# Four products of a block's last state, spread over the first step of the next block

## The chip, the cores and the metric

The kernel runs on one core of one Trainium2 chip. The metric is the device time of one execution in microseconds (us). A core has five engines that run side by side and wait for each other by semaphores: TensorE (matrix products, "PE" in the profile, its weight loads "PEld"), VectorE ("DVE"), ScalarE ("ACT"), GpSimd ("POOL") and SyncE ("SP"), from whose queue nearly all transfers of this kernel are issued, one after the other. Each engine takes its instructions in program order, so one that waits holds up all behind it.

## The reference, cut to what matters

Two layers follow each other; the change is in the second one, a gated recurrence. Its input `x` has 8 rows in time and 2048 columns that are independent of each other (the recurrence calls them a batch), of width 512.

```
def step(c, xt):
    ft = sigmoid(xt @ wf.T + c @ uf.T + bf)
    it = sigmoid(xt @ wi.T + c @ ui.T + bi)
    gt = tanh(xt @ wc.T + c @ uc.T + bc)
    c = ft * c + it * gt
    return (c, None)
c_final, _ = lax.scan(step, c0, x)
h = tanh(einsum('tbi,oi->tbo', x, wo) + c_final @ uo.T + bo)
out = x + layernorm(h)
```

The state after the last step, `c_final`, enters every row of the output by one product with `uo`. That product, plus the bias `bo`, is what the change moves. The first layer (a state-space convolution, a gelu and a layer norm) takes the time up to about 680 us and is not touched.

## The kernel before

**Blocks and steps.** The 2048 columns are cut into four blocks `q` of 512. Each block runs through 8 steps `t`, so there are 32 steps `n = 8q + t`, one after the other. A step has eight units: two `z` units (the product of `x` with `wo`, independent of the state), then six gate units (gates 1, 2, 0 for the first half of the outputs, then gates 1, 2, 0 for the second half). The products are computed by a scheme with seven instead of eight block products, in pairs of f16 numbers (three matmuls for each f32 product). At `t = 0` the initial state is the same for all columns, its product is part of the bias, and the gate units have no state part: 24 matmuls in a unit's first half and 18 in its second. At `t > 0` a gate unit has twice as many.

**Order.** The order of every engine's work is written by hand. Slot `sl` of step `n` calls `part_a` of its unit (first 24 or 48 matmuls, then sums from the result tile by ScalarE and VectorE: `u2`, `c22`, `u[:, 2:4]`), then whatever was put at place `p = 16n + 2 sl`, then `part_b` of the unit before (the other matmuls, then either the copy of a `z` result to memory, L973 to L980, or the gate functions on ScalarE, L987, and for gate 0 the new state in `state`, L1007 to L1020), then whatever was put at `p + 1`. In every step but the first the second half of `z1` is held back by one slot (`late`). The state is written as f16 pairs `cf0`, `cf1`, for the two halves; `cf1` is the last thing that a step makes, and falls in the next step's first slots.

**Result tiles.** `pu` has three tiles `u` that units take in turn, so a unit's first matmul waits until an older unit's results have been read.

**Side work, with its places.** `prep` (load `y` and `xr`, layer norm statistics, scale, sum, store) prepares two steps of the input of one 128-column chunk; it holds the single tiles with the tags `y` and `wl`. 60 preparations are spread over the steps by `when`. `turn` loads the next step's input, normalises it, transposes it on TensorE (L485) and writes its forms `xf`. `head` makes the output rows of the block before, five or four to a step with `t > 0`: load `z`, add the state's product `u`, tanh, statistics, normalise, add `x1`, store. The last heads of a block reach into the next block's first step. `tail` does the same for the last block after the last step.

**The product of the last state.** `last(q - 1)` is put in the first step of block `q`. Its `load` (place 5) issues the bias `bo` and four weight tiles `uw`; its `sums` (place 7) takes two `u` tiles, runs all 60 matmuls (4 products, 512 wide, for the four chunks `cj`: 12, 12, 18 and 18) and has VectorE add the bias (L1056); its `store` (place 8) writes the four results, which the heads read back. After the last step `last(3)` runs the same without a store.

## Time and profile before

| | us |
|---|---|
| median of 3 runs (2947.64 to 2950.56) | 2949.14 |
| the profiled execution | 2952.36 |
| its span | 2950.6 |
| ordinary step at t > 0, blocks 1 to 3 (1627.96 to 1694.21) | 66.25 |
| first step of block 1 (1223.61 to 1297.96) | 74.35 |
| first step of block 2 (1760.45 to 1837.12) | 76.67 |
| first step of block 3 (2299.07 to 2376.22) | 77.15 |
| idle of TensorE ahead of the product, by a DMA, block 1 | 8.0 |

Steps are measured from the start of the first matmul of `z0` to the next step's. In the profile's rows, "x" gives a count of instructions, the mean duration is in ns, and after the bar stand the idle time of the engine just before such instructions and what ended it. Matmuls overlap, so a matmul's duration is longer than the time from one start to the next; where that matters, starts are compared.

### The profile page before, as it was taken

Reading aid. Unit: us, or ns where it says so; the run is one execution under the profiler, and the core shown is the slowest. Engines: PE = TensorE matmul, PEld = TensorE weight load, DVE = VectorE, ACT = ScalarE, POOL = GpSimd, SP = SyncE. Lnnn points to the kernel's source line nnn. Section 1 sums busy time; section 2 is a strip of 40 time slices with the busy share of each in tenths; the row PEclk is TensorE's granted clock in tenths of the full one; section 3 lists DMA queues with packets and bytes.
Section 4 is the critical chain, followed back from the end, with each engine's and each line's share of the span. In section 5 each row is a group of like instructions: output and inputs, shape, how many; then the busy total and the mean of one; then the engine's idle time right before and its main releaser. Section 6 shows DMA issues by size and latency. Waiting matters only on the chain.

```text
span 2950.6 us, 60067 instructions
## 1 busy us (share of the span) xinstructions
PE 2600.0 (88%) x23940; PEld 2262.3 (77%) x23940; DVE 2068.4 (70%) x4260; ACT 1487.0 (50%) x3076; POOL 1115.1 (38%) x1484
## 2 busy tenths in 40 slices
PE   4678888875899999899999997999999899999970
PEld 3367777764788888778888885888888688888850
DVE  8868778736666676667777776777777577777637
ACT  8856666633344444434555543445454345454425
POOL 5756677612111111114434331343433224333217
PEclk8789999986999999999999998999999999999985
DMA  6877887794433223334454444455545344543227
GB/s 240 287 223 248 252 259 245 236 269 164 129 94 80 72 72 89 102 107 132 138 148 136 129 119 122 108 154 150 153 121 136 108 125 136 138 129 113 82 107 278
DMA packets 517762, 452.15 MB, mean 153 GB/s; under 512 B 285926, under 2 KB 397032, under 8 KB 512488
## 3 DMA queue, kind: packets, MB, share of 16 engines
q1 hardware_dynamic: 517048, 447.79, 51.1%
q8 instruction: 187, 3.06, 0.4%
q14 instruction: 95, 0.78, 0.1%
q10 hardware_dynamic: 432, 0.52, 0.1%
HBM read 296.46 MB, written 151.78 MB: 152 GB/s over the span
## 4 chain that ended last, share of the span: by engine, by line
PE 55%; DVE 11%; ACT 4%; DMA 4%; issue 1%; POOL 1%; SPq 1%; POOLq 0%; ACTq 0%; DVEq 0%
PE u L921 51%; PE pt L485 2%; DVE cd L1008 1%; ACT xa L907 1%; DVE gate L1007 1%; DVE stx L462 1%; DVE u L963 1%; DMA zz<-z_d 1%; PE u L450 1%; DMA uw<-uo_d 1%; PE u L451 1%; PE u L452 1%; DVE gate L1011 1%; DMA z_d<-zc 1%; DVE sth L462 1%
## 5 line engine op out<-in xcount | busy, mean ns | idle before, releaser
L921 PEld LDWEIGHTS <-w 128*128 128x128 f16 x15120 | 1485.3, 98 | 204.8 <-issue 15.0
L921 PE MATMUL u<-xf,w 128*128 128x256 f16 x8064 | 953.3, 275 | 23.8 <-DVE u L963 10.5
L921 PE MATMUL u<-cf,w 128*128 128x256 f16 x7056 | 825.2, 273 | 0.0
L987 ACT ACTIVATE gate<-u,bias 128x512 f32<-128x512 f32 (+1 forms) x384 | 200.9, 575 | 267.6 <-PE u L921 267.6
L921 PE MATMUL u<-w,xf 128*128 128x256 f16 x2688 | 311.7, 274 | 8.7 <-DVE u L963 8.7
L1094 POOL TENSOR_TENSOR x1r<-x1r,zr 128x512 f32<-128x512 f32 x96 | 124.5, 1297 | 487.9 <-ACT zr L1093 400.3
L882 POOL TENSOR_TENSOR xr<-y,xr 128x512 f32<-128x512 f32 x120 | 150.9, 1279 | 399.7 <-ACT y L881 399.7
L921 PEld LDWEIGHTS <-xf 128*128 128x128 f16 x2688 | 264.0, 98 | 41.2 <-DVE u L963 9.5
L960 DVE TENSOR_TENSOR u2p<-u2p,u 128x256 f32<-128x256 f32 x256 | 107.0, 418 | 237.3 <-ACT u2p L959 236.8
L959 ACT ACTIVATE u2p<-u 128x256 f32<-128x256 f32 x256 | 96.4, 376 | 316.3 <-PE u L921 316.3
L471 POOL TENSOR_TENSOR rsy<-rsy,nhalf 128x2 f32<-128x2 f32 (+1 forms) x68 | 48.5, 714 | 513.5 <-DVE rsy L465 502.6
L963 DVE TENSOR_TENSOR u<-u,u2p 128x512 f32<-128x512 f32 x256 | 178.9, 699 | 8.8
L639 POOL TENSOR_TENSOR u<-xg,u 128x512 f16<-128x512 f32 x104 | 128.6, 1240 | 124.6 <-ACT u L637 124.0
L633 POOL TENSOR_TENSOR xg<-xg,mu 128x512 f32<-128x512 f32 x112 | 162.3, 1456 | 9.5 <-DMA xg<-in_xr 9.5
L102 DVE TENSOR_TENSOR x<-pxt,x 128x256 f16<-128x256 f32 x240 | 99.9, 418 | 71.0 <-ACT x L101 69.9
L101 ACT ACTIVATE xf<-pt 128x512 f16<-128x512 f32 x124 | 60.8, 490 | 164.5 <-DVE ts L495 117.5
L1018 ACT ACTIVATE cf<-gate 128x512 f16<-128x512 f32 x128 | 80.7, 630 | 121.6 <-DVE gate L1011 103.1
L462 DVE BATCH_NORM_STATS2 sty<-y 128x6 f32<-128x512 f32 x120 | 76.8, 682 | 91.4 <-DMA y<-y_d 91.4
L101 ACT ACTIVATE x<-pxt 128x256 f16<-128x256 f32 x240 | 91.3, 381 | 80.7 <-PE pxt L659 74.6
L452 PE MATMUL pyt<-u,t 128*128 128x128 f16 (+2 forms) x544 | 124.7, 229 | 4.9 <-POOL u L615 4.9
L450 PE MATMUL pyt<-u,t 128*128 128x128 f16 (+2 forms) x544 | 121.6, 224 | 6.4 <-ACT y L738 3.4
L1076 POOL TENSOR_TENSOR zr<-zr,ur 128x512 f32<-128x512 f32 x96 | 122.1, 1272 | 9.1 <-DMA zr<-z_d 8.9
(349 smaller groups left out, 5279.5 us busy)
## 6 DMA issues: line engine op xcount, KB each, us to landing
xs<-in_rr SPq DMA_DIRECT2D x32, 1024.0 KB, 6.6
t<-kpad SPq DMA_DIRECT2D x32, 1024.0 KB, 5.7
xa<-x_d SPq DMA_DIRECT2D x124, 256.0 KB, 3.8
xr<-in_r SPq DMA_DIRECT2D x61, 512.0 KB, 6.5
x_d<-xr SPq DMA_DIRECT2D x61, 512.0 KB, 3.2
y_d<-y SPq DMA_DIRECT2D x30, 1024.0 KB, 7.5
y<-y_d SPq DMA_DIRECT2D x60, 512.0 KB, 5.7
xg<-in_xr SPq DMA_DIRECT2D x28, 1024.0 KB, 8.6
```

What stands on the lines that cost most here:

```text
L101: S.activation(hi, src, AF.Copy)
L450: T.matmul(out, lhsT=w(0), rhs=x(0), start=start, stop=False)
L452: T.matmul(out, lhsT=w(0), rhs=x(1), start=False, stop=stop)
L462: V.bn_stats(st[:, i], v)
L633: Q.tensor_tensor(xg, xg, bc(mu1), ALU.subtract)
L639: (V if g == 2 else Q).tensor_tensor(u[:, js, 1], xg, u[:, js, 0], ALU.subtract)
L882: Q.tensor_tensor(xv, yv, xv, ALU.add)
L921: T.matmul(u[:, d], lhsT=w(f, b, i == 1, k), rhs=x(f, b, i == 2, k), start=opens and bank not in seen, stop=stop and j == len(n) - 1, skip ...
L963: V.tensor_tensor(u[:, 2:4], u[:, 2:4], u2[:, None].to_broadcast([P, 2, BP]), ALU.add)
L987: act = lambda o, s_, b: S.activation(o, s_, AF.Tanh, scale=gsc[kind], bias=b)
L1076: Q.tensor_tensor(s_["z"], s_["z"], us_[c], ALU.add)
L1094: Q.tensor_tensor(s_["x"], s_["x"], s_["z"], ALU.add)
```

## The change

The product is cut into four, one for each chunk, each with a `u` tile of its own (except after the last step, where two chunks share one). Loads, four products and four results get places of their own: the weights at -2, which is in the last slot of the step before; the bias at 4; the products at 3, 5, 7 and 13; the results at 5, 7, 9 and 14; the store at 15. The weights now lie in the tiles of the preparations (tags `wl` and `y`), in two loads. The result is copied by ScalarE from the `u` tile, ScalarE scales the bias once, and GpSimd adds it; after the last step VectorE still adds it in place.

For this, the first step of a block has no preparations; the others are spread over the steps with `t > 0`, at new places: three of them at `t = 3` and `t = 5`, two at the others. In the first step of blocks 1 to 3 the turn is put earlier (0 to 10 in place of 2 to 13), and `z1` is no longer held back.

```diff
     def last(q):
-        end, uws, uo = q == NQB - 1, [], []
+        end, uws, uo, us = q == NQB - 1, [], [], {}
         def load():
-            bo = FT.tile([P, H], F32, name="bo", tag="x1r", bufs=2)
-            dma(out=bo, in_=a["bo"])
             if end:
                 u4 = FE.tile([P, KT, 2, H], F16, name="uw", tag="xf")
                 dma(out=u4, in_=uo_d.rearrange("k p a m -> p k a m"))
                 uws.extend(u4[:, k] for k in range(KT))
+                return
+            for i, (pool, tag) in enumerate(((FJ, "wl"), (FE, "y"))):
+                u2 = pool.tile([P, 2, 2, H], F16, name="uw", tag=tag)
+                dma(out=u2, in_=uo_d[2 * i : 2 * i + 2].rearrange("k p a m -> p k a m"))
+                uws.extend(u2[:, k] for k in range(2))
+        def load_b():
+            bo = FT.tile([P, H], F32, name="bo", tag="x1r", bufs=2)
+            dma(out=bo, in_=a["bo"])
+            uws.append(bo)
+        def sums(cj):
+            cf, i, cs = cfs[q, NB - 1], cj // 2, slice(cj % 2 * P, (cj % 2 + 1) * P)
+            if end and cj % 2:
+                u = us[cj - 1]
             else:
-                for k in range(KT):
-                    uw = FT.tile([P, 2, H], F16, name="uw", tag="zr", bufs=4)
-                    dma(out=uw, in_=uo_d[k])
-                    uws.append(uw)
-            uws.append(bo)
...
+                u = pu.tile([P, 4, BP], F32, name="u").rearrange("p (a b) c -> p a (b c)", a=2)
+            us[cj] = u
...
+        def out(cj):
+            p_ = us[cj][:, cj % 2]
+            if end:
+                V.scalar_tensor_tensor(p_, uws[KT], SW, p_, ALU.mult, ALU.add)
+                us_[QC * q + cj] = p_
+            else:
+                u_ = FT.tile([P, H], F32, name="u_", tag="zr", bufs=4)
+                S.activation(u_, p_, AF.Copy)
+                if cj == 0:
+                    S.mul(uws[KT], uws[KT], SW)
+                Q.tensor_tensor(u_, u_, uws[KT], ALU.add)
+                uo.append(u_)
...
-        return (load, sums) if end else (load, sums, store)
+        one = lambda f, cj: lambda: f(cj)
+        return [load, load_b] + [one(f, cj) for cj in range(QC) for f in (sums, out)] + ([] if end else [store])
...
-    PA, PB = (5, 7, 8, 10, 11), (12, 16, 17, 19, 20)
...
-    when += [(n, p) for n in range(2, len(steps)) for p in (PA, PB)]
+    PF, PL = ((1, 3, 4, 5, 6), (7, 9, 10, 11, 12)), ((5, 7, 8, 10, 11), (11, 13, 14, 15, 16))
+    PT = PF + ((13, 16, 17, 19, 20),)
+    when = [(0, p) for p in ((0, 2, 3, 4, 5), (5, 7, 8, 9, 10), (11, 13, 14, 15, 16))] + [(1, p) for p in PT]
+    for n, (q, t) in enumerate(steps):
+        if n > 1 and t:
+            when += [(n, p) for p in (PT if t in (3, 5) else PL if t in (4, 6) or n == 2 else PF)]
...
+        if q and t == 0:
+            put(last(q - 1), b, (-2, 4, 3, 5, 5, 7, 7, 9, 13, 14, 15))
         if n + 1 < len(steps):
+            ps = ((2, 5, 6, 7, 8), (9, 10, 11, 12, 13))
+            if t == 0:
+                ps = ((0, 1, 2, 3, 5), (6, 7, 8, 9, 10)) if n else ((0, 1, 2, 3, 4), (5, 6, 8, 9, 11))
             for i in range(2):
-                put(turn(*steps[n + 1], i), b, (((2, 5, 6, 7, 8), (9, 10, 11, 12, 13)) if n else ((0, 1, 2, 3, 4), (5, 6, 8, 9, 11)))[i])
+                put(turn(*steps[n + 1], i), b, ps[i])
...
-        if q and t == 0:
-            put(last(q - 1), b, (5, 7, 8))
...
-                late = n and sl == 2
-                if sl == 3 and n:
+                late = n and t and sl == 2
+                if sl == 3 and n and t:
                     finish(zs[1], p + 1)
                     before = gs[0]
```

More of the change, by code (lines that the diff above doesn't have):

```diff
@@ L1032, in load @@
                 uws.extend(u4[:, k] for k in range(KT))
-            else:
-                for k in range(KT):
-                    uw = FT.tile([P, 2, H], F16, name="uw", tag="zr", bufs=4)
-                    dma(out=uw, in_=uo_d[k])
-                    uws.append(uw)
-            uws.append(bo)
-        def sums():
-            cf = cfs[q, NB - 1]
-            uu = [pu.tile([P, 4, BP], F32, name="u").rearrange("p (a b) c -> p a (b c)", a=2) for _ in range(2)]
-            for cj in range(QC):
-                i, cs = cj // 2, slice(cj % 2 * P, (cj % 2 + 1) * P)
-                ps = [(k, b) for k in range(KT) for b in (((FB11,) if i == 0 else (FB11, FT1)) if k < 2 else ((FB21,) if i == 0 else (FB22,)))]
-                for n, (k, b) in enumerate(ps):
-                    mm3(uu[i][:, cj % 2], lambda l: cf[k % 2][:, b, l, cs], lambda l: uws[k][:, l],
-                        start=(n == 0), stop=(n == len(ps) - 1))
-            for cj in range(QC):
-                p_ = uu[cj // 2][:, cj % 2]
-                if end:
-                    us_[QC * q + cj] = u_ = p_
-                else:
-                    u_ = FT.tile([P, H], F32, name="u_", tag="zr", bufs=4)
-                    uo.append(u_)
-                V.scalar_tensor_tensor(u_, uws[KT], SW, p_, ALU.mult, ALU.add)
@@ new lines, in load @@
+                return
[11 more added lines that the diff above has]
+                u = us[cj - 1]
+            else:
+                u = pu.tile([P, 4, BP], F32, name="u").rearrange("p (a b) c -> p a (b c)", a=2)
+            us[cj] = u
+            ps = [(k, b) for k in range(KT) for b in (((FB11,) if i == 0 else (FB11, FT1)) if k < 2 else ((FB21,) if i == 0 else (FB22,)))]
+            for n, (k, b) in enumerate(ps):
+                mm3(u[:, cj % 2], lambda l: cf[k % 2][:, b, l, cs], lambda l: uws[k][:, l],
+                    start=(n == 0), stop=(n == len(ps) - 1))
@@ L1164, in s4_gated_block @@
     chunks = [(g, cj) for g in range(1, len(pairs)) for cj in (0, 2, 1, 3)]
-    PA, PB = (5, 7, 8, 10, 11), (12, 16, 17, 19, 20)
-    when = [(0, (0, 2, 3, 4, 5)), (0, (5, 7, 8, 9, 10)), (0, (11, 13, 14, 15, 16)),
-            (1, (1, 3, 4, 5, 6)), (1, (7, 9, 10, 11, 12)), (1, (13, 16, 17, 19, 20))]
-    when += [(n, p) for n in range(2, len(steps)) for p in (PA, PB)]
+    PF, PL = ((1, 3, 4, 5, 6), (7, 9, 10, 11, 12)), ((5, 7, 8, 10, 11), (11, 13, 14, 15, 16))
[4 more added lines that the diff above has]
+            when += [(n, p) for p in (PT if t in (3, 5) else PL if t in (4, 6) or n == 2 else PF)]
     for n, (q, t) in enumerate(steps):
```

## The prediction

> **What bounds the kernel now.** I read the page first, then the steps of the recurrence one by one (from the first matmul of a step's unit z0 to that of the next step), then the chain of waits and the timelines inside the steps that the diff touches.

> ```profile
> span 2950.6 us, 60067 instructions
> PE 2600.0 (88%) x23940; PEld 2262.3 (77%) x23940; DVE 2068.4 (70%) x4260; ACT 1487.0 (50%) x3076; POOL 1115.1 (38%) x1484
> L921 PE MATMUL u<-cf,w 128*128 128x256 f16 x7056 | 825.2, 273 | 0.0
> ```

> TensorE is the busiest engine, and its recurrent products never wait. Next, busy time by stretch: the three first steps of blocks 1 to 3, then an ordinary step (columns: stretch, length, then PE, PEld, DVE, ACT, POOL busy, clock, DMA).

> ```profile
> 1223.61:1297.96 74.35, 59.61 (x432) 44.43 (x430) 43.73 (x88) 27.11 (x56) 10.50 (x16) 0.89 0.38 110
> 1760.45:1837.12 76.67, 58.85 (x432) 43.97 (x430) 45.86 (x93) 28.71 (x58) 13.75 (x22) 0.89 0.44 130
> 2299.07:2376.22 77.15, 59.24 (x433) 44.16 (x430) 46.18 (x93) 28.92 (x58) 13.76 (x22) 0.89 0.45 129
> 1627.96:1694.21 66.25, 66.20 (x607) 59.23 (x605) 49.37 (x101) 32.86 (x64) 24.23 (x37) 1.00 0.47 132
> ```

> The ordinary step is TensorE's own work, at full clock (588 matmuls of 109.2 ns and two groups of transposes make 66.0). The first steps take 8 to 11 us more with 30% fewer matmuls. What they wait for is in the chain (start, length, what) and in TensorE's timeline; the bracket is the idle time before a row and its releaser.

> ```profile
> 1243.98 3.35 SPq L869
> ...
> 1247.37 0.47 SPq L1028
> ...
> 1247.88 4.42 DMA uw<-uo_d
> 1252.30 0.14 issue
> 1252.43 0.59 PE u L450
> 1253.02 0.43 PE u L451
> ```

> ```profile
> 1279.87 6.41 PE L921 MATMUL u<-xf,w 128*128 128x256 f16 x42 [2.09 <-ACT gate L987]
> 1290.74 1.82 PE L485 MATMUL pt<-cst,xa 128*128 128x128 f32 x8 [4.46 <-ACT xa L907]
> 1292.35 5.78 PE L921 MATMUL u<-xf,w 128*128 128x256 f16 x42
> ```

> ```profile
> 2357.63 2.78 PE L921 MATMUL u<-xf,w 128*128 128x256 f16 x24 [1.80 <-ACT gate L987]
> 2360.86 2.14 PE L921 MATMUL u<-xf,w 128*128 128x256 f16 x18 [0.46 <-DVE u L963]
> 2368.50 1.97 PE L485 MATMUL pt<-cst,xa 128*128 128x128 f32 x8 [5.50 <-ACT xa L907]
> ```

> The weights queue behind a preparation's loads on SP, and TensorE stands for 8 us. Then it runs slow: products start every 0.43 us at first, every 0.2155 later. A stop of 2.09 is followed by 42 matmuls in 6.2 instead of 4.6; a stop of 1.80 is not (24 in 2.8).

> **TensorE's floor in such a step.** Full-rate matmuls start every 109.2 ns (24 in 2.62 us). 336 of the step and 18 of the state before make 38.7; 60 wide ones at 215.5 ns, 12.9; 16 transposes in two groups of 0.87, 1.7: together 53.3. The three steps stand 21.1, 23.4 and 23.9 over it, 68.3 in all.

> **The new order, first boundary.** I call the units z0, z1, g1 to g6, their halves A (24 matmuls, 2.6) and B (18, 2.0), the products p0 to p3 (2.6, 2.6, 3.9, 3.9), the transposes T0, T1. The program of the changed kernel has TensorE do A z0, B of the old g6, A z1, B z0, p0, A g1, B z1, p1, T0, A g2, B g1, p2, A g3, B g2, A g4, T1, B g3, A g5, B g4, p3, A g6, B g5, next z0. Each p takes one of three result buffers, so p1 waits for z1's, p2 for g1's, A g4 for g2's, p3 for g3's, A g6 for g4's, each used shortly before. I walk from the step's start with the durations of this trace.
> p0: the last cf of the old state is done at 14.0 (1237.61), and p0 would be over at 13.7: it ends at 14.5, 0.8 lost. A g1 to 17.1. VectorE then has the turn's statistics (1.6) ahead of z1's sums (2.05), done 17.6: B z1 to 19.6, 0.5 lost. ScalarE stands behind the same statistics, as GpSimd needs 1.6 more for the scale (1284.65 to 1286.2): norm 17.2 to 18.6, g1's copy 18.9, z1's copy 20.5; p1 from 20.6 to 23.2, 1.0 lost. T0 24.0, A g2 26.7, B g1 28.6. The forms of T0 hold ScalarE 5.0 (1273.46 to 1278.48), to 29.2; g2's copy and g1's gates 1.8: p2 from 31.1, 2.45 lost, and as that is over 2.09, a slow stretch: 2.15 (ten products at 0.43 for 0.2155). p2 ends 37.1, A g3 39.7, B g2 41.7, its gates 42.9: A g4 from 42.95, 1.25 lost. Then T1, B g3, A g5, B g4 to 53.0. The forms of T1 begin on VectorE after g4's sums at 48.1, leave ScalarE 4.3 later, g3's gates end at 53.85: p3 from 53.95, 0.95 lost, to 57.8. The state of g3 keeps ScalarE until 58.75 (5.05 from VectorE's L1005, as 1284.56 to 1289.62), then g5's copy and g4's gates to 60.5: A g6 from 60.55, 2.7 lost, slow stretch 2.15, to 65.3; B g5 67.3. The next z0 takes p3's buffer, already copied.
> Sum: 53.3 + 9.65 lost + 4.3 slow = 67.3 for 74.35: 7.0 gained.

> **Second and third boundary.** Heads of the block before run in here too. z1's copy has one output tile, which must have been stored for z0; the trace has that wait:

> ```profile
> 1244.86 0.38 ACT L973 ACTIVATE zt<-u 128x256 f32<-128x256 f32 x1 [3.93 <-DMA z_d<-zt]
> ```

> On SP that store now follows a head's store (GpSimd's sum done at 15.1, landing 2.5 after issue) and the bias load, which waits for this landing: issued 17.9, the z store 18.4, its second part landed 3.0 after its issue, 21.9. p1 starts 2.3 later, 3.2 lost instead of 1.0, and a third slow stretch: 4.4 more, 71.7 for 76.67 and 77.15: 5.0 and 5.4 gained. Three boundaries: 17.4.

> **Edits costed at nothing.** The weights (two loads where there were four) take the tiles of the last preparation of the step before, behind its store on SP, and are issued about 8 us before the first step, needed 11 after its start; 5.3 to landing (DMA rows). Without that cover: up to 5.3 each. GpSimd's four sums are 1.3 each (L1094) on an engine busy 10.5 to 13.8; p3's ends at about 67.7, and SP, with the u stores, has the next step's first preparation behind it; VectorE reads that about 13 us into the step, and landing takes 5.7. ScalarE's four copies (0.59, L974) and one scaling (0.62, L1079) are in the walk; VectorE loses four sums of 0.70. Two preparations leave each first step, and later steps take three where they took two: VectorE 49.4 + 1.9 (two statistics of 0.68, small ones) of 66.2, GpSimd some 4 more on 28. Bounds: none, by the ordinary step above, or 8 us per such step, as in the slower rival; I take none, since TensorE's sums run one unit ahead.
> At the end the weights are issued ahead of the bias (0.43 sooner), the second and fourth product wait for VectorE's sum in their tile (0.9 each), and one sum fewer follows the last (0.7): 0.7 lost.
> So 2949.1 (the median; the profiled execution took 2952.4 around its span of 2950.6) - 17.4 + 0.7 = 2932.

> [...] The row: 1.80 and 1.93 us idle (at 2357 and 1818) left the clock full, 2.09 and 2.64 (at 1279 and 816) did not. [...] I go by the row.

> **Rivals.** (1) The clock holds through these stops, or copies come sooner than walked: 4.3, 6.4 and 6.4 less on top, 34.5 in all, 2915; all 68.3 gone would be 2881, against which stand five buffer waits per step. (2) The gain is used up in the step: each stop of about 1 us that grows past 2.1 costs 1.1 and a slow stretch, 3.2; two at each boundary undo it, 2950. For it: the first of the three steps has 14.9 idle of its 21.1, so already loses 6 by the clock. Against: the copies are short. (3) Slower: the denser preparations. One in an ordinary step finds its rows late:

> ```profile
> DVE sty L462 <- DMA y<-y_d: 4.1, 1, 4.1
> ```

> Three such in a step with heads: VectorE 51.3 + 12.3, and 10.8 for its other waits in that step (5.2 and 5.6 on ScalarE), 74.4 of 66.2: 8.2 over, in five steps 41, so 2973. It outweighs the gain from 3.3 over per step (16.7 by five). Against: the first of them is loaded right at the step's start and read after the state, 13 us later; before this, one of two had this wait and cost TensorE nothing. (4) The products wait for late weights after all: 5.3 on three boundaries, 2948.

> **How the numbers follow.** 0.2% (5.9 us) is about what a measurement tells from no change. The forecast 0.58 (2922 to 2943 alone), rival 1 0.2, rivals 2 and 4 0.11, rival 3 0.11: faster 0.78, same 0.11, slower 0.11. Time 2932; range 2908 to 2951, from 7 under the first rival's 2915, for copies sooner than walked, to no gain; it leaves out rival 3 and what lies under 2908.

> **What would show it.** First steps of 67 and 72 us; no wait on uw; stops ahead of p1, p2, p3 and A g6 ended by ScalarE, clock above 0.89; ordinary steps still 66.2. Wrong: ordinary steps with three preparations longer than 67, or first steps under 64 or over 74.

## The result, and the profile after

The changed kernel takes 3064.43 us (median of 4 runs, 3061.47 to 3065.35) against 2949.85 before: a ratio of 1.0388 (95% interval 1.037 to 1.0406), 115 us slower where 17 faster were forecast. The page of the changed kernel, first the engines, then groups of instructions:

```profile
span 3062.7 us, 60022 instructions
...
PE 2622.4 (86%) x23940; PEld 2276.1 (74%) x23940; DVE 2062.9 (67%) x4248; ACT 1499.4 (49%) x3091; POOL 1119.5 (37%) x1496
...
L921 PE MATMUL u<-cf,w 128*128 128x256 f16 x7056 | 825.2, 273 | 0.0
...
L485 PE MATMUL pt<-cst,xa 128*128 128x128 f32 x496 | 82.3, 317 | 110.2 <-ACT xa L907 109.8
```

The same group of the kernel before, which the prediction did not show:

```profile
L485 PE MATMUL pt<-cst,xa 128*128 128x128 f32 x496 | 74.3, 289 | 34.1 <-ACT xa L907 33.1
```

The engines' work hardly grew: ScalarE is busy 12.4 us longer, with 15 more instructions, and TensorE 22.4 longer with the same 23940 matmuls, at a mean granted clock of 0.94 for 0.948. The rest is waiting: TensorE stands 76 us longer ahead of the turn's transposes, which wait for ScalarE's norm of `xa`. Where this happens is seen by stretch (stretch, length, then PE, PEld, DVE, ACT, POOL busy, clock, DMA): the three first steps, then the ordinary steps n = 10 and n = 3, and n = 14.

```profile
1237.25:1306.91 69.66, 56.46 (x432) 42.47 (x430) 40.20 (x77) 27.56 (x57) 7.43 (x10) 0.95 0.10 35
1814.06:1887.41 73.35, 57.85 (x432) 42.78 (x430) 41.14 (x80) 28.97 (x59) 10.93 (x15) 0.93 0.19 60
2387.94:2463.15 75.21, 58.89 (x433) 42.99 (x431) 41.12 (x80) 28.97 (x59) 10.94 (x15) 0.91 0.18 58
1377.23:1454.67 77.44, 69.00 (x606) 61.07 (x604) 49.28 (x103) 34.12 (x66) 26.75 (x42) 0.93 0.44 123
893.92:964.38 70.46, 67.81 (x606) 60.43 (x604) 44.57 (x88) 29.76 (x58) 12.34 (x18) 0.98 0.41 105
1671.31:1737.55 66.24, 66.19 (x606) 59.21 (x604) 49.72 (x104) 32.88 (x64) 24.42 (x36) 1.00 0.47 130
```

The first steps gain 4.7, 3.3 and 1.9, 10 in all for a forecast of 17.4. The loss is in ordinary steps, which I had left at 66.2: n = 10 takes 77.4 (66.30 before), n = 3 takes 70.5 (65.94), n = 14 is untouched. Step by step, t = 1, 2, 3, 5, 7 are longer, by 4.5 in block 0 and by 5.4 to 11.1 in blocks 1 to 3, sixteen steps in all, ten of them at t = 2, 3, 5 and 7 of blocks 1 to 3 (the expectations below count fifteen and nine; the last preparation is in n = 28, and nothing is lost behind it); t = 4 and t = 6 are not. It makes no difference whether a step has two preparations (n = 10) or three (n = 11, 75.8). What the longer steps share is the second preparation's places, (7, 9, 10, 11, 12). Summed over the 26 ordinary steps from n = 2 to 30 the loss is 120.9 (1836.8 for 1715.9), and 120.9 - 10.0 + 1.2 at the end is the 112 by which the span grew.

Inside the step n = 10 of the changed kernel (it starts at 1377.23): TensorE, GpSimd and ScalarE around the step's second transposes, T1 (each fence is the timeline of one engine; the bracket is the idle time before a row and its releaser).

```profile
1431.16 2.13 PE L921 MATMUL u<-cf,w 128*128 128x256 f16 x18
1441.73 1.97 PE L485 MATMUL pt<-cst,xa 128*128 128x128 f32 x8 [8.44 <-ACT xa L907]
1443.49 4.80 PE L921 MATMUL u<-xf,w 128*128 128x256 f16 x24
```

```profile
1437.02 2.54 POOL L882 TENSOR_TENSOR xr<-y,xr 128x512 f32<-128x512 f32 x2 [9.50 <-ACT y L881]
1439.52 0.71 POOL L471 TENSOR_TENSOR rsx<-rsx,nhalf 128x2 f32<-128x2 f32 x1
```

```profile
1416.37 0.66 ACT L492 ACTIVATE b<-pt 128x256 f32<-128x256 f32 x2 [5.80 <-DMA z_d<-zc]
...
1432.11 0.42 ACT L1018 ACTIVATE cf<-cd 128x256 f16<-128x256 f32 x1 [6.90 <-DVE cd L1008]
...
1436.14 1.50 ACT L881 ACTIVATE y<-y,nmy,rsy 128x512 f32<-128x512 f32 x2
...
1440.86 1.52 ACT L907 ACTIVATE xa<-xa,nmx,rsx 128x512 f32<-128x512 f32 x2 [1.73 <-POOL nmx L476]
```

Read backwards: T1 waits for the norm of `xa`, this for the turn's scale on GpSimd (L471), which is ready to run when VectorE's statistics end at 1429.7 but starts at 1439.52. In front of it GpSimd holds the preparation's sum (L882); this waits for ScalarE's norm of `y` (L881), which is queued behind the state's copies `cf` (L1018). So at place 11 a preparation that nobody hurries for stands ahead of a turn that TensorE needs. The stop of 8.44 is followed by a slow stretch (24 matmuls in 4.6). And everything here is late already: the first copy of T0's forms, `b`, started only after 5.8 idle, since it lies in the tile of `zc` (tag `un`; the code calls it `b1`) and the store of `z1`'s `zc` (a part of the unit's result) had not landed. Why it had not is in SP's queue:

```profile
1403.30 0.32 SPq L885 DMA_DIRECT2D x_d<-xr  x1
1403.73 0.54 SPq L867 DMA_DIRECT2D y<-y_d  x1
1406.53 2.76 SPq L869 DMA_DIRECT2D xr<-in_r  x1
...
1410.85 0.43 SPq L980 DMA_DIRECT2D z_d<-zc  x1
```

The first preparation stores its sum, the second loads into the same tile, waits 2.2 for that store to land, and `z1`'s store comes behind, 33.6 into the step.

The kernel before has the same step from 1362.58 on; GpSimd, ScalarE and SP there:

```profile
1406.73 2.51 POOL L882 TENSOR_TENSOR xr<-y,xr 128x512 f32<-128x512 f32 x2 [5.70 <-ACT y L881]
1409.80 0.72 POOL L471 TENSOR_TENSOR rsx<-rsx,nhalf 128x2 f32<-128x2 f32 x1 [0.55 <-DVE rsx L465]
```

```profile
1398.01 0.66 ACT L492 ACTIVATE b<-pt 128x256 f32<-128x256 f32 x2 [2.10 <-DMA z_d<-zc]
...
1405.85 1.51 ACT L881 ACTIVATE y<-y,nmy,rsy 128x512 f32<-128x512 f32 x2
...
1412.14 0.42 ACT L1018 ACTIVATE cf<-cd 128x256 f16<-128x256 f32 x1 [1.59 <-DVE cd L1008]
```

```profile
1392.24 0.54 SPq L980 DMA_DIRECT2D z_d<-zc  x1
...
1409.68 0.54 SPq L867 DMA_DIRECT2D y<-y_d  x1
```

The norm of `y` runs ahead of the state's copies, the sum is over when the turn's scale is due, and the scale waits for VectorE alone. `z1`'s store goes out 29.7 into the step, ahead of the second preparation's load. T1 starts at 1418.52 without a stop.

### The profile page after: what moved, and what is told of

It is laid out like the page before. It is cut to its first block, busy times and chain, and to the rows that moved or that the text cites. A ratio compares the mean times of both kernels' runs of the same rounds, so it can differ in the third digit from the quotient of the medians.

```text
span 3062.7 us, 60022 instructions
## 1 busy us (share of the span) xinstructions
PE 2622.4 (86%) x23940; PEld 2276.1 (74%) x23940; DVE 2062.9 (67%) x4248; ACT 1499.4 (49%) x3091; POOL 1119.5 (37%) x1496
## 5 line engine op out<-in xcount | busy, mean ns | idle before, releaser
L921 PEld LDWEIGHTS <-w 128*128 128x128 f16 x15120 | 1492.0, 99 | 213.7 <-issue 18.4
L921 PE MATMUL u<-xf,w 128*128 128x256 f16 x8064 | 963.4, 277 | 26.2 <-ACT gate L987 12.2
L921 PE MATMUL u<-cf,w 128*128 128x256 f16 x7056 | 825.2, 273 | 0.0
L987 ACT ACTIVATE gate<-u,bias 128x512 f32<-128x512 f32 (+1 forms) x384 | 201.1, 575 | 278.5 <-PE u L921 278.5
L921 PE MATMUL u<-w,xf 128*128 128x256 f16 x2688 | 311.2, 274 | 9.8 <-DVE u L963 9.6
L921 PEld LDWEIGHTS <-xf 128*128 128x128 f16 x2688 | 263.9, 98 | 42.4 <-DVE u L963 10.2
L882 POOL TENSOR_TENSOR xr<-y,xr 128x512 f32<-128x512 f32 x120 | 153.5, 1300 | 312.1 <-ACT y L881 311.9
L471 POOL TENSOR_TENSOR rsy<-rsy,nhalf 128x2 f32<-128x2 f32 (+1 forms) x68 | 48.3, 711 | 492.9 <-DVE rsy L465 481.6
L963 DVE TENSOR_TENSOR u<-u,u2p 128x512 f32<-128x512 f32 x256 | 179.0, 699 | 8.8
L485 PE MATMUL pt<-cst,xa 128*128 128x128 f32 x496 | 82.3, 317 | 110.2 <-ACT xa L907 109.8
L485 PEld LDWEIGHTS pt<-cst,xa 128*128 128x128 f32 x496 | 66.4, 163 | 119.6 <-ACT xa L907 118.0
L102 DVE TENSOR_TENSOR x<-pxt,x 128x256 f16<-128x256 f32 x240 | 100.2, 419 | 71.1 <-ACT x L101 69.9
L1018 ACT ACTIVATE cf<-gate 128x512 f16<-128x512 f32 x128 | 80.7, 630 | 121.6 <-DVE gate L1011 103.2
L493 DVE TENSOR_TENSOR ts<-pt,b 128x512 f32<-128x512 f32 x62 | 42.7, 689 | 133.0 <-ACT b L492 130.7
L1018 ACT ACTIVATE cf<-cd 128x256 f16<-128x256 f32 (+1 forms) x128 | 66.0, 515 | 132.5 <-DVE cd L1008 132.5
```

The lines of the kernel that those rows point to most:

```text
L102: V.tensor_tensor(lo, src, hi, ALU.subtract)
L485: T.transpose(pt[h][:, k], xa[h][:, k * P : (k + 1) * P], ident)
L882: Q.tensor_tensor(xv, yv, xv, ALU.add)
L921: T.matmul(u[:, d], lhsT=w(f, b, i == 1, k), rhs=x(f, b, i == 2, k), start=opens and bank not in seen, stop=stop and j == len(n) - 1, skip ...
L963: V.tensor_tensor(u[:, 2:4], u[:, 2:4], u2[:, None].to_broadcast([P, 2, BP]), ALU.add)
L987: act = lambda o, s_, b: S.activation(o, s_, AF.Tanh, scale=gsc[kind], bias=b)
```

## The experiments

Theory C: T1 is late by the order at place 11. Theory C2 adds the late `b`. Rivals: three preparations are too many (T), SP's queue is too full for the weights (S), the spread itself (P). Fifteen kernels ran; all lengths below are from their traces, one each, and ratios from timed runs beside the kernel before, whose own median was between 2949.85 and 2956.17; so kernels of different rounds are compared by their ratios. "Ordinary" is the sum of the 26 steps above, "first" that of n = 8, 16 and 24, "start" the time until step n = 2 begins.

| kernel | median | ratio (95%) | start | ordinary | first |
|---|---|---|---|---|---|
| before | 2949.85 | 1 | 828.0 | 1715.9 | 228.2 |
| changed | 3064.43 | 1.0388 (1.037 to 1.0406) | 828.0 | 1836.8 | 218.2 |
| e1 sum at 10 | 2979.0 | 1.0082 (1.0063 to 1.0101) | 826.1 | 1753.2 | 219.0 |
| e2 turn called first | 3013.77 | 1.0206 (1.019 to 1.0222) | 813.6 | 1802.4 | 217.3 |
| e3 places alone | 3056.36 | 1.0341 (1.0326 to 1.0357) | 828.8 | 1843.6 | 205.7 |
| e4 load behind z1 | 3047.75 | 1.0311 (1.0293 to 1.0328) | 830.2 | 1842.3 | 196.4 |
| e5 b in ts | 3015.76 | 1.0209 (1.0196 to 1.0222) | 830.1 | 1802.3 | 202.2 |
| e6 e1, e4 and e5 | 2933.63 | 0.9929 (0.9917 to 0.9941) | 824.5 | 1726.8 | 203.9 |
| e7 the same, product undivided | 2932.34 | 0.993 (0.9918 to 0.9943) | 823.5 | 1727.4 | 199.9 |
| e8 before, b in ts | 2948.98 | 0.998 (0.9971 to 0.9988) | 830.5 | 1715.1 | 225.1 |
| e9 e7, early first turns | 2933.7 | 0.9944 (0.9928 to 0.9961) | 819.3 | 1727.5 | 205.3 |
| e10 e2 and e5 | 2943.33 | 0.9973 (0.9963 to 0.9984) | 813.8 | 1750.3 | 196.4 |
| e11 e9, norm at 11 | 2919.19 | 0.9894 (0.9879 to 0.9909) | 821.5 | 1710.3 | 205.4 |
| e12 e6, norm at 11 | 2909.31 | 0.9859 (0.9844 to 0.9874) | 823.9 | 1710.1 | 194.9 |
| e13 e12 and e2 | 2902.3 | 0.9834 (0.9819 to 0.9848) | 813.1 | 1709.9 | 197.7 |
| e14 late preparation | 2948.54 | 0.9991 (0.9981 to 1.0) | 820.9 | 1727.1 | 218.8 |
| e15 e7, norm at 11 | 2914.04 | 0.987 (0.9854 to 0.9887) | 823.9 | 1711.1 | 201.8 |

**The sum one place earlier.** All five parts of the second preparation move, each by one place.

```diff
-    PF, PL = ((1, 3, 4, 5, 6), (7, 9, 10, 11, 12)), ...
+    PF, PL = ((1, 3, 4, 5, 6), (6, 8, 9, 10, 11)), ...
```

> Changed kernel, but the second preparation of a step with places (7, 9, 10, 11, 12) stands at (6, 8, 9, 10, 11), so that its sum comes one place earlier, ahead of the state and of the turn's scale; all else, the steps with three preparations too, is kept. Theory C (the sum stands at place 11 ahead of the turn's scale on GpSimd, waits for ScalarE behind the state's copies, and so the second transposes come late): the 15 lengthened ordinary steps return to 66.2 us or, in block 0, 65.9; they hold 121 us of the changed kernel's 3064, so 2938 to 2952. Rival T (three preparations in a step are too many): the steps with three (n = 3, 5, 11, 13, 19, 21, 27) keep their 51 us, 2990 to 3000. Rival S (the preparations' loads hold up SyncE's queue, with the weights behind them): these places are denser on SyncE, not looser, so 3060 or more.

Block 0 is back at 65.9 in every step; in blocks 1 to 3, 37 of the 121 us stay: n = 10 is 72.9, n = 14 still 66.25. T falls: steps with three preparations recover like those with two (n = 11 and n = 13 are 69.6). So does S as it was put, since the new places are denser on SP. C holds for the larger part (2979 measured, 2938 to 2952 expected) but does not explain the rest: there T1 still waits (3.98 in n = 10), now with GpSimd's sum and scale done 6 us before ScalarE's norm starts. That led to `b`. As the whole preparation moved, this run alone does not tell GpSimd's queue from ScalarE's; the next one does.

**The turn called before the preparation, at the same places.**

```diff
         for i in range(2):
             put(turn(*steps[n + 1], i), b, ps[i])
+        for (gp, cj), (n_, p) in zip(chunks, when):
+            if n_ == n:
+                put(prep(*pairs[gp], cj), b, p)
```

(The same three lines are taken out ahead of the weights' and the turn's.)

> Changed kernel, all places kept; only within one place the turn's part is called before the preparation's, so that at place 11 GpSimd gets the turn's scale ahead of the preparation's sum. ScalarE's order (the preparation's norm at place 11, the turn's at 12) stays. Theory C, with GpSimd's order as the whole cause: the transposes no longer wait for the sum, and all 121 us return, about 2943. Theory C with both queues in it: in step n = 10 the turn's norm started at 1440.86, behind a scale that started at 1439.52; with the scale done early it can start at 1437.6, where ScalarE ends the preparation's norm, so 3.3 of the 8.4 us of waiting go; 3.3 in 12 steps and 1 to 3 in the three of block 0 is some 40 to 50, 3015 to 3025. Rivals T and S: nothing changes, 3060 to 3068.

34 us of the ordinary steps return, by nothing but the order in GpSimd's queue: in the longer steps place 11 is the only one where the two calls put work on the same engine. Another 14 return at the start: some 4 in n = 1, which has the same places, and 7.6 ahead of the very first transposes, for a reason that e13 shows. So the total comes close to the 3015 to 3025 expected partly by luck: that had 40 to 50 in the ordinary steps and nothing at the start. Block 0 (66.0) is free, and t = 1 nearly so (66.5 to 67.0 for 70 in the changed kernel and 64.5 before); at t = 2, 3, 5, 7 little is won, since ScalarE still does the preparation's norm first, and all of it late.

**The places without the spread.** The kernel before, with the changed kernel's list of preparations.

> Kernel before, with the product in one place, its weights, the turns and the held-back z1 as they were; only the list of the preparations' places is the changed kernel's (none in a first step, three at t = 3 and 5). Theory C: the ordinary steps are lengthened as in the changed kernel, some +121 us; the first steps, without a preparation's loads ahead of the weights (3.35 us of SyncE at 1243.98), may give back 3 to 4 each: 3055 to 3072. Rival P (the product's own spread, its weights in the tiles of the preparations, lengthens the ordinary steps): these steps stay at 66.2, 2935 to 2955.

The ordinary steps lose 127.7, even more than with the whole change: P falls. And the first steps, with the product in one place, gain 22.5, more than twice what the change gains, where I had expected 3 to 4 in each. Of the change's parts, the one that helped most was taking the preparations out of the first step.

**The first step's own stop.** Its timeline in the changed kernel, SP and then ScalarE:

```profile
1261.27 0.79 SPq L896 DMA_DIRECT2D xa<-x_d  x2
...
1263.11 0.43 SPq L980 DMA_DIRECT2D z_d<-zc  x1
```

```profile
1266.55 0.66 ACT L492 ACTIVATE b<-pt 128x256 f32<-128x256 f32 x2 [7.58 <-DMA z_d<-zc]
```

The turn's second load, at place 6, waits 7.3 on SP until T0, the first transposes, has read its tile (1261.3), and `z1`'s store stands behind it.

```diff
-    ps = ((0, 1, 2, 3, 5), (6, 7, 8, 9, 10)) if n else ...
+    ps = ((0, 1, 2, 3, 5), (7, 7, 8, 9, 10)) if n else ...
```

> Changed kernel; only the turn's second load in the first steps of blocks 1 to 3 is moved from place 6 to 7, so that it stands behind z1's store on SyncE. Theory D (the load waits for the first transposes to free its tile, done 1261.5; z1's store is issued behind it at 1263.1 and lands at 1266.5; the transposes' first copy on ScalarE needs z1's tile zc back): the copy starts some 4 us sooner, the stop ahead of p2 falls from 7.0, 7.1 and 8.3 to some 3, and 12 to 13 us go, 3050 to 3054; if the stops come under 2.1, the slow stretches go too, 3045 to 3048. Rival (the stop is the length of the transposes' forms on ScalarE, taken too short by me): at most 1 us per first step, 3060 to 3065.

The stop ahead of p2 falls from 7.0, 7.1 and 8.3 to 2.1, no slow stretch follows it, and the first steps give 21.8. They are 9.3 shorter than in e3, with the undivided product; between e6 and e7 below that lead is gone. The ordinary steps are not helped.

**`b` in a tile of its own time.**

```diff
-        b1 = FJ.tile([P, 2, 2, P], F32, name="b1", tag="un")
         ts = FJ.tile([P, 4, 2, P], F32, name="ts", tag="ws")
+        b1 = ts[:, 2:4]
```

> Changed kernel, all places kept; only the transposes' first copy b, which shared one tile (tag un) with z1's result zc and so waited until z1's store had landed, goes into the half of ts that is written later. Theory C2 (two causes in an ordinary step: the sum at place 11, and a late landing of z1's store that makes the forms of T0, and with them the state, some 4 us late): in blocks 1 to 3 about 4 us go in each of the nine steps with two or more preparations at t = 2, 3, 5, 7, some 36 in all; block 0, without heads, keeps its +4.5 per step; the first steps fall as in the run with the later load, 22. So 3000 to 3015. Rival (b's wait is hidden in ordinary steps, the sum alone counts): only the first steps gain, 3040 to 3048.

34.5 go from the ordinary steps, some 36 expected, and 16 from the first, 22 expected; block 0 keeps its 4.5 per step. So both halves of C2 are there, each alone worth a part.

**All three, and the same without the spread.**

> Changed kernel with the second preparation at (6, 8, 9, 10, 11), the turn's second load of a first step at 7, and b in ts. Theory C2: ordinary steps 66.2 (three preparations or two), first steps 63, 66.7 and 66.7 as in the run with the later load: 74.35 + 76.67 + 77.15 - 196.4 = 31.8 under the kernel before, 0.7 of it given back at the end: 29 to 34 below it, a ratio of 0.988 to 0.990. Rival T (three preparations still cost where all else is mended): 1 to 3 us in each of seven steps, 10 to 25 below.

> As the kernel before with the product undivided in one place, its weights in four tiles and z1 held back; the preparations at the mended places (none in a first step), b in ts. What the spread itself is worth is the difference to the run with all three edits. If the spread pays little once the preparations are out of the first steps: first steps of 66.8, 71.5 and 67.4 (as with the places alone), 22 below the kernel before, 7 to 10 over the run with all three. Rival (the spread is what pays): 0 to 10 below the kernel before.

110 of the 121 us are gone, and the kernel beats the one before by 0.7%, 21 us instead of 29 to 34. T is not why: n = 10 with two preparations and n = 11 with three are both 67.1. In thirteen steps T1 still waits 0.65 to 1.07, and the clock took some 7 us more in the first steps than in e4 (64.7, 69.7, 69.5 for 63.0, 66.7, 66.7, with p2's stop at 2.1 in both but a slow stretch behind it in e6 alone). With the product undivided the time is the same: the expected 7 to 10 us for the spread did not appear.

**The kernel before with `b` in `ts`.**

> Kernel before with only b in ts. If the shared tile cost nothing in the kernel before (its ordinary steps are TensorE's own work): within 0.1% of it, at most 2 us less in each first step. Rival (it costs there too, hidden in the stops ahead of T1 of the first steps): 8 to 15 less.

0.2% faster, 3.1 us of it in the first steps and 0.8 in the ordinary ones: twice the 0.1% I had expected at most. The shared tile was nearly free as long as the stores came early.

**Both queues, no place moved.** e2 and e5 together, with every place of the changed kernel.

> Changed kernel with all its places kept: within one place the turn is called before the preparation, and b lies in ts. Each alone left 3014 to 3016. Theory C2 (those two waits are the whole loss of the ordinary steps): all of them at 66.2 to 67.2, or up to 1.5 more where ScalarE still does the preparation's norm ahead of the turn's, first steps 63 to 70 as with b in ts: 2930 to 2950. Rival (a third cause, such as three preparations or loads in the way): steps of 69 and more remain, 2965 to 3000.

As C2 has it, with the reserve: 86 of 121 return, and the steps at t = 2, 3, 5, 7 of blocks 1 to 3 are 68.5 to 70.2, where T1 waits 2.1 behind the preparation's norm on ScalarE. The three of 70.2 are beyond the reserve, by the clock: their stop is the same 2.12, but at n = 15 it is followed by 3.41 us at a granted clock of 0.50, and at n = 11 (68.5) the clock stays full.

**The first turns early, with the product undivided.**

> As the run with the product undivided and the preparations at mended places; only the turn of the first steps of blocks 1 to 3 is put early, at the changed kernel's places with its second load at 7: (0, 1, 2, 3, 5) and (7, 7, 8, 9, 10). Theory E (what is left in those steps is not the product but the turn: T1 waits 6.45 us for its norm, which stands behind the state's copies on ScalarE, and a slow stretch follows): 6.4 to 8.1 less in each first step, so 56 to 58, 61 to 62 and 59 to 60, 19 to 24 us in all. Rival (the stop moves on to the gates behind the forms, as in the spread order): 0 to 8 in all.

Theory E failed, and so did its rival: the stop of 6.45 ahead of T1 went, and 4.0 to 4.5 came ahead of T0 and 5.2 to 5.7 at the end of the step, where matmuls wait for VectorE's sums (L963). The first steps got 5.4 longer.

**The second turn's norm one place earlier.**

```diff
-    ps = ((2, 5, 6, 7, 8), (9, 10, 11, 12, 13))
+    ps = ((2, 5, 6, 7, 8), (9, 10, 11, 11, 13))
```

> As the run with the early turns in the first steps, and in every ordinary step the second turn's norm is called at place 11 instead of 12, ahead of the heads' norm and tanh on ScalarE. Theory: the 0.7 us by which T1 still waits in twelve ordinary steps of 67.13 goes, steps of 66.25, 10 us less than that run. Rival (T1 waits for the state's copies, not for the heads): no change.

> As the run with all three edits on the changed kernel, so with the product spread, plus the second turn's norm at place 11. Ordinary steps as in the run before this one; first steps 63 to 70 as they were. If the spread is worth nothing even so, it ends level with or above the undivided product with early turns: 2918 to 2926 against 2895 to 2905. Rival (spread pays once the turns are right): it ends below.

Both lose 17 in the ordinary steps, more than the 10 expected: n = 10 of e12 now has no stop at all and is shorter than before the change, at full clock.

```profile
1348.13:1414.06 65.93, 65.93 (x606) 59.27 (x604) 49.21 (x104) 33.81 (x66) 27.28 (x42) 1.00 0.51 145
```

e12 ends below e11, against my expectation, but by e11's first turns, which e9 had made worse.

**Why `z1`'s store was late, what the spread is worth, and the start.** For e14:

```diff
-    PF, PL = ((1, 3, 4, 5, 6), (7, 9, 10, 11, 12)), ...
-    PT = PF + ((13, 16, 17, 19, 20),)
+    PN = ((1, 3, 4, 5, 6), (6, 8, 9, 10, 11))
+    PF, PL = ((1, 3, 4, 5, 6), (9, 12, 13, 14, 15)), ...
+    PT = PF + ((15, 17, 18, 19, 20),)
```

(`PN` serves t = 7.)

> Changed kernel with b still in zc's tile; the second preparation at t = 1, 2, 3 and 5 stands at (9, 12, 13, 14, 15), its load behind z1's store on SyncE and its sum behind the turn; the third at (15, 17, 18, 19, 20); at t = 7 the second at (6, 8, 9, 10, 11). Theory S2 (z1's store lands late because the second preparation's load, which must wait until the first's sum is stored from the same tile, stands ahead of it on SyncE): the steps at t = 1, 2, 3, 5 return to 66.2 to 67 though b keeps the shared tile, those at t = 7 stay at 67 to 71, the first steps as in the changed kernel: 2948 to 2960. Rival (a second preparation in that stretch holds z1's store wherever its load stands, or the third does): steps of 69 and more at t = 2, 3, 5 remain, 2970 or more.

> As the spread product with all mended (b in ts, second preparation at 6, second load at 7, second turn's norm at 11), and within one place the turn called before the preparation. In both runs with that order the time from the start to step n = 2 was 813.5 and 813.9 us, in the others 819 to 830. Theory (the order frees the turn of the very first step from a preparation's sum): 10 less than the same kernel without it, 2896 to 2903. Rival (those 10 us hang on the other places of those two runs): 2906 to 2912.

> The product undivided, preparations mended, b in ts, the turns of the first steps where the kernel before has them, and only the second turn's norm at 11. From the sums of the runs: ordinary steps as in the two runs with that norm (17 less than the run with the undivided product without it), first steps 199.9 for 194.9: 2912 to 2918, so that the spread, with everything around it mended on both sides, is worth 3 to 8 us. Rival (the undivided product with the late turn loses in the first steps too, as with the early turn): 2919 or more.

e14 returns t = 1, 2, 3 and 5 to 64.2 to 66.25 in all blocks, with `b` still in `zc`'s tile; t = 7 stays at 67.3 and 68.6, as said, and some steps at t = 4 and 6 are longer, one of them 71.1. The waits of `b` for that store show it (total, times, longest): the kernel before, the changed one, e14.

```profile
ACT b L492 <- DMA z_d<-zc: 24.1, 15, 2.7
```

```profile
ACT b L492 <- DMA z_d<-zc: 57.6, 15, 7.6
```

```profile
ACT b L492 <- DMA z_d<-zc: 25.1, 7, 7.4
```

In the changed kernel the waits at t = 2, 3, 5 and 7 are 3.3 to 5.8 us each; in e14 none is left at t = 1, 2, 3 and 5, and the rest is in the first step of block 1 (7.4) and at t = 4, 6 and 7. So it is the order on SP, not the number of preparations. e13 is the fastest, 1.7% under the kernel before: in its very first step the first transposes wait 7.77 where they waited 15.19 in e12. But not for the reason in its expectation, a preparation's sum on GpSimd: in e12 VectorE's statistics stand 15.30 for the load of `xa`. SP's queue at the start, e12 and then e13 (the transposes below them, in the same order):

```profile
694.11 0.62 SPq L867 DMA_DIRECT2D y<-y_d  x1
...
697.73 0.87 SPq L896 DMA_DIRECT2D xa<-x_d  x2
```

```profile
691.65 0.32 SPq L896 DMA_DIRECT2D xa<-x_d  x1
692.79 0.62 SPq L867 DMA_DIRECT2D y<-y_d  x1
```

```profile
706.37 1.97 PE L485 MATMUL pt<-cst,xa 128*128 128x128 f32 x8 [15.19 <-ACT xa L907]
```

```profile
697.66 1.97 PE L485 MATMUL pt<-cst,xa 128*128 128x128 f32 x8 [7.77 <-ACT xa L907]
```

In e12 the preparation's load waits 3.5 for an older store from its tile, with the turn's load behind it; in e13 the turn's load goes first. So the number expected came out, and its mechanism did not: it is SP again. All runs but e2, e10 and e13, the three with this order, have a wait of 14.8 or more there. The kernel before calls the two in the same order as e12 and waits 14.8; that the same swap would help it was not tried. e15 and e12 differ by 6.9 in the first steps of one trace each, where the clock alone moves some 3 us a step, and the intervals of their ratios overlap: the spread is worth 0.1% or so, or nothing.

## Why the prediction was wrong

**The step that failed** is "Edits costed at nothing", in its sentence "Bounds: none, by the ordinary step above, or 8 us per such step ...; I take none, since TensorE's sums run one unit ahead." I had walked the new order through the first steps, and not through one ordinary step, though most of the 60 preparations got new places there; for those I added up the busy time of VectorE and GpSimd. The cover I named, sums that run one unit ahead, is not what the new places hit: they hit GpSimd's queue at place 11 and SP's queue ahead of `z1`'s store. The term was 0 and measured 120.9. The bound of 8 us had the right size (4.5 to 11.1), but went to five steps, those with three preparations, instead of sixteen. The trace of before even held a step with these places, n = 1, and its stop of 2.64 ahead of T1 stands in the prediction, used for the clock alone.

**Rival 3** (0.11) had the side and not the mechanism. It let VectorE wait for late rows; that wait fell, from 91.4 us in 27 cases before to 26.7 in 8 after, and three preparations were no worse than two. It was 91 us short.

**The first steps.** The walk held at most stops (block 1, walked against measured): p0 0.8, 0.34; B z1 0.5, 0.35; p1 1.0, 1.01; A g4 1.25, 1.14; p3 0.95, 0.71; A g6 2.7, 2.56; p1 of block 2 3.2, 3.35. No wait on `uw`, as said, and the end lost 1.2 for 0.7. It failed at p2: 2.45 walked, 7.0 measured, because I took the forms' 5.0 on ScalarE and not the wait of their first copy for a store that I had put on SP in the wrong order. With that wait gone (e4) the stop is 2.1 and the gain 31.8 instead of the forecast 17.4.

**The slow stretches.** "I go by the row" did not hold. The stop of 2.56 ahead of A g6, three times in the changed kernel, left the clock full, where I had charged 2.15 for 2.09 and more; that is why the first steps beat the walk behind p2. It was luck: stops of one length went both ways, 2.13 in e6 with a slow stretch behind it and 2.12 in e4 without, and the last section shows what the traces hold of it. Of rival 1 this part was there (the 14.9 idle that it names is 14.7 by its row, 74.35 less 59.61, which changes nothing); rivals 2 and 4 were not.

## What to carry to other kernels

When side work moves to other places of a hand-written order, walk the whole step with it on every in-order queue, not only the engine that it keeps busy: an instruction that waits holds whatever stands behind it (here the turn's scale, ready on GpSimd for 9.8 us behind the preparation's sum), and a place shared by two pipelines is decided by which is called first (34 us of the ordinary steps in e2). Two results that share one tile couple their engines through the landing of a store (`b` waited 57.6 us in all for it in the changed kernel, 25.1 in e14); look for "ended by a DMA" on an engine that only copies. And split a change by its parts: here taking the preparations out of three steps was worth 22 us in them, the spread that gave the change its name close to nothing.

## What the runs showed of the hardware

The same stop at the same place was followed by a slow stretch in one run and not in another. Ahead of p2 in block 1, e6 and then e4:

```profile
1251.22 0.38 PE L450 MATMUL u<-uw,cf 128*128 128x512 f16 x1 [2.13 <-ACT gate L987]
...
1251.81 0.63 PE L452 MATMUL u<-uw,cf 128*128 128x512 f16 x1
1252.24 0.63 PE L450 MATMUL u<-uw,cf 128*128 128x512 f16 x1
```

```profile
1270.52 0.38 PE L450 MATMUL u<-uw,cf 128*128 128x512 f16 x1 [2.12 <-ACT gate L987]
...
1270.95 0.38 PE L452 MATMUL u<-uw,cf 128*128 128x512 f16 x1
1271.16 0.38 PE L450 MATMUL u<-uw,cf 128*128 128x512 f16 x1
```

Products start every 0.43 us in the one and every 0.2155 in the other, so 1.7 us hang on it; in e13 the first step of block 2 is 68.1 for e12's 65.1, with stops equal to 0.2, so nearly all by the clock: the stop ahead of p1 is 3.30 in e13, with products every 0.43 behind it, and 3.13 in e12, with products every 0.2155. In the changed kernel a stop of 2.56 (ahead of A g6) left the clock full, one of 2.65 (n = 3) did not (24 matmuls in 3.5 behind it instead of 2.6).

| trace | clock 0.50 in the next window | idle in these | clock still 1.00 | idle in these |
|---|---|---|---|---|
| before | 8 windows | 2.09 us or more | 563 windows | 1.93 us or less |
| changed | 22 windows | 2.15 us or more | 559 windows | 1.94 us or less |

The same sum over all 17 traces has 167 windows ahead of a fall, 166 of them with 2.01 us of idle time or more and one with 1.88, and 9640 ahead of none, with 2.01 or less. This is what these traces hold; what else a fall may take was not measured. The two stops above, window by window (stretch, length, PE busy, clock, DMA; idle is the length less PE busy), e6 and then e4:

```profile
1248.07:1251.48 3.41, 1.28 (x12) 1.00 0.01 3
1251.48:1254.89 3.41, 3.41 (x10) 0.50 0.20 77
```

```profile
1265.45:1268.86 3.41, 2.94 (x27) 1.00 0.45 151
1268.86:1272.28 3.42, 1.76 (x9) 1.00 0.01 2
1272.28:1275.69 3.41, 3.41 (x23) 1.00 0.20 77
```

In e6 the whole stop of 2.13 falls in one window; in e4 it is cut into 0.47 and 1.66, as the 2.56 ahead of A g6 in block 1 of the changed kernel is into 1.06 and 1.50.
